# Softmax denominators of a causal self attention: summed on GpSimd and multiplied once a group

## The chip, the cores and the metric

The kernel runs on one core of one Trainium2 chip. The metric is the device time of one execution in microseconds (us). The engines are named as the profile names them: PE (TensorE, matmuls; PEld are its weight loads), DVE (VectorE), ACT (ScalarE), POOL (GpSimd) and SP (SyncE, which issues DMAs).

## The reference, cut to what matters

The reference is a two-layer Perceiver-like block on x of 512 rows by 512 columns. Each layer is a cross attention to 8192 context rows, a self attention over the 512 rows and a mixture of eight experts. The change touches the first layer's self attention alone:

```python
def _L0_attn_ref(x, w_qkv, b_qkv, w_out, b_out):
    ...
    qkv = x @ w_qkv + b_qkv
    q, k, v = jnp.split(qkv, 3, axis=-1)
    ...
    scores = jnp.einsum('bhid,bhjd->bhij', q, k) * attn_scale
    scores = jnp.where(j >= i, scores, -jnp.inf)
    attn = jax.nn.softmax(scores, axis=-1)
    out = jnp.einsum('bhij,bhjd->bhid', attn, v)
    out = out.transpose(0, 2, 1, 3).reshape(B, S, H)
    return out @ w_out + b_out
```

There are 16 heads of 32 columns. Query row i sees the keys j >= i only. The softmax needs, for each query and head, the sum of the weights exp(score - maximum) over its keys: the denominator.

## The kernel before

All is in 32-bit floats. The 16 heads are worked in four groups g of four heads (GH), the 512 keys in four tiles of 128. `self_attention0` works the tiles of a group in places i = 0 to 3, where place i holds key tile t = 3 - i. Since a query sees only keys at or behind it, tile t serves the queries 0 to (t + 1) * 128, so the widths w at places 0 to 3 are 512, 384, 256 and 128.

The steps of a group are closures. An order written out by hand, the string given to `in_order`, says which step's instructions are emitted next; each engine then works its own queue in order. A scheduler may still shift single instructions a little against this order.

- **q, k** (`query`, `key`, L1612 and L1616): projections on PE, with ACT adding the bias.
- **M g.t** (`maxima`): scores of a query tile on PE (L1683, and the causal mask added by a matmul at L1688), then on DVE the row maxima (L1692). **S** (`shift_of`) makes of them the shifts (DVE L826 and L829, PE transposes L835, DVE copy L839).
- **W g.i** (`weighted`): for four heads the scores with keys along partitions (PE L1670) and the shift subtracted by a small matmul (L800); ACT takes the exponentials into the tile pT (L1714); POOL sets the weights above the diagonal to zero in the last 128 columns (`affine_select`, L1716). Then it calls `sums` for the place before.
- **sums** (L1704): the matmuls of the weights of one place. With the values as weights loaded on PE they add to `acc`, with a matrix of ones (`ones32`) to `den`. The four heads of a batch write four blocks of 32 partitions. `acc` and `den` are one PSUM bank each, for the whole group; the places accumulate there.
- **F g** (`finish`): `sums` of the last place, then on ACT a copy of `acc` to `o` (L870) and the logarithm of `den` to `d` (L872).
- **D g** (`quotient`): ACT exp(-d) (L876), POOL o times d (L877), ACT adds the value bias (L880).
- **O g.j** (`outputs`): the output projection of two query tiles (PE L889), added to x by DVE (L895).
- **V** (`part`): a piece of another stage's work, the value projection of the second cross attention (PE L1548, ACT copy L1553). These pieces are spread through the order.
- **E, T**: group 3 is worked by query tiles and not by key tiles. It keeps its own denominators (L1743) in both kernels.

The tile pT has four buffers. PSUM has eight banks: six rotate among all short-lived tiles, scores, projections and transposes (`tile_s`: a new tile waits until the sixth before it has been read), and `acc` and `den` hold one each.

The part of the order that matters here (W0.2 is place 2 of group 0):

```python
"q0 k0 q1 M0.0 k1 M0.1 V M0.2 M0.3 q2 S0.0 M1.0 k2 M1.1 V S0.1 W0.0 M1.2 V W0.1 M1.3 "
"W0.2 W0.3 F0 S1.0 q3 D0 M2.0 M2.1 V S1.1 k3 M2.2 W1.0 O0.0 M2.3 W1.1 O0.1 "
"M3.0 V W1.2 M3.1 W1.3 F1 S2.0 M3.2 V D1 M3.3 S2.1 V W2.0 W2.1 S3.0 W2.2 "
"O1.0 W2.3 F2 S3.1 D2 O1.1 W3.0 V W3.1 V E3 O2.1 W3.2 V O2.0 E2 T3 W3.3 E1 T2 V E0 T1 "
```

Of the kernel before, what the change touches and what calls it, by code (L numbers as in the profile page):

```python
# [11 lines left out]
F32 = mybir.dt.float32  # L12
# [4 lines left out]
AF = mybir.ActivationFunctionType  # L17
ALU = mybir.AluOpType
# [3 lines left out]
P = 128  # L22
S = 512
D = 512
H = 16
HD = 32
S2 = 8192
NT = S // P
NC = D // P
NG = 4  # L30
GH = 4
# [3 lines left out]
E = 8  # L35
# [30 lines left out]
def tile_perceiver(  # L66
# [5 lines left out]
    nc = tc.nc  # L72

    def tile_pool(**kw):

        return tc.tile_pool(reuse_waits="tile", **kw)
# [38 lines left out]
    with tile_pool(name="begins", bufs=1) as tmp, tile_pool(name="beginsps", bufs=1, space=PSUM) as tps:  # L115
        t = tmp.tile([1, NCHUNK, CH // P], F32, name="brow")
        nc.gpsimd.iota(
            t, pattern=[[NC * CH // P, NCHUNK], [1, CH // P]], base=0, channel_multiplier=0,
# [11 lines left out]
    for i in range(2):  # L130
        t = const.tile([P, NT, GH, HD], BF16, name=f"mparts{i}")
# [9 lines left out]
    steps = const.tile([P, S], F32, name="steps")  # L141
# [21 lines left out]
    for i, caps in enumerate((CAPS0, CAPS1)):  # L163
        t = const.tile([P, 2, E], F32, name=f"rooms{i}")
# [5 lines left out]
    for i, name in enumerate(("L0_ffn_router", "L1_ffn_Wg")):  # L170
        t = const.tile([P, NC, E], F32, name=f"router{i}")
# [729 lines left out]
    def in_order(order, steps, k):  # L901


        shifts = {}
        for step in order.split():
            name, *n = step[0], *[int(v) for v in step[1:].split(".") if v]
            if name == "S":
                g, i = n
                if i == 0:
                    shifts[g] = k.shift_of(g)  # L910
                shifts[g][i]()
            elif name == "D":
                k.quotient(*n)
            elif name == "O":
                k.outputs(n[0], range(2 * n[1], 2 * n[1] + 2))
            else:
                steps[name](*n)
# [685 lines left out]
    def early_turns(k, tiles, to):  # L1603

        for t in tiles:
            turn(None, None, t, to, 0, held=True, tp=k.tile_s((P, NC, P), "lnt"))
# [11 lines left out]
    def self_attention0(pool, to, ahead=None):  # L1618
        with ExitStack() as st:
            psum = st.enter_context(tile_pool(name="s0ps", bufs=3, space=PSUM))  # L1620
            pacc = st.enter_context(tile_pool(name="s0acc", bufs=1, space=PSUM))
# [14 lines left out]
            vN = pool.tile([P, NT, D], F32, name="vNs", tag="vNs", bufs=1)  # L1636
            k = in_quads(pool, psum, pacc, qT, lambda: wo, bv, lambda: pool)
            k.rowwise = "whole"
            k.last = 0
            k.between = lambda: early_turns(k, (3, 2), to)  # L1640
            last = []

            def query(g):
                project(k, lambda c: wq[:, c, g * P : (g + 1) * P], xnT, 0, qT[:, g, :], bq[:, g : g + 1], SCALE)
# [19 lines left out]
            def scores(g, i):  # L1664
                t = NT - 1 - i
                w = (t + 1) * P
                tiles = [k.tile_s() for _ in range(GH)]
                for h in range(GH):
                    r = slice(HD * h, HD * (h + 1))
                    nc.tensor.matmul(  # L1670
                        tiles[h][:, 0:w], lhsT=kT[r, g, t * P : (t + 1) * P], rhs=qT[r, g, 0:w],
                        start=True, stop=False,
                    )
                for h in range(GH):
                    k.subtract(g, h, tiles[h][:, 0:w], w)
                return tiles, w
# [17 lines left out]
            def sums():  # L1694

                if not last:
                    return
                g, i, w, pT = last.pop()
                if i == 0:
                    k.begin(g)  # L1700
                t = NT - 1 - i
                for what in range(2):
                    for h in range(GH):
                        nc.tensor.matmul(  # L1704
                            k.sums[g][what][HD * h : HD * (h + 1), 0:w],
                            lhsT=k.ones32 if what else vN[:, t, g * P + HD * h : g * P + HD * (h + 1)],
                            rhs=pT[:, h, 0:w], start=(i == 0), stop=(i == NT - 1),
                        )

            def weighted(g, i):  # L1710
                tiles, w = scores(g, i)
                pT = pool.tile([P, GH, S], F32, name="pT", tag="pT", bufs=4)
                for h in range(GH):
                    nc.scalar.activation(pT[:, h, 0:w], tiles[h][:, 0:w], AF.Exp)  # L1714

                nc.gpsimd.affine_select(  # L1716
                    out=pT[:, :, w - P : w], in_=pT[:, :, w - P : w], compare_op=ALU.is_ge, fill=0.0,
                    base=0, pattern=[[0, GH], [-1, P]], channel_multiplier=1,
                )
                sums()  # L1720
                if g < NG - 1:
                    last.append((g, i, w, pT))
                else:
                    pTs[NT - 1 - i] = pT

            def finish(g):
                sums()
                k.finish(g)

            pTs = {}  # L1730

# [18 lines left out]
            def tail(t):  # L1750
                k.outputs(NG - 1, (t,))

            in_order(
# [5 lines left out]
                {"q": query, "k": key, "M": maxima, "W": weighted, "F": finish, "E": end, "T": tail, "V": part}, k,  # L1759
            )  # L1760

    def self_attention1(pool, to):

        W = S + 2 * PAD
        with ExitStack() as st:
# [75 lines left out]
            def finish(g):  # L1841
# [13 lines left out]
                k.finish(g, 2 if g == NG - 1 else 1)  # L1855

            in_order(
                "q0 k0 M0 q1 S0.0 k1 S0.1 M1 q2 S0.2 S1.0 W0 k2 S1.1 M2 F0 S1.2 q3 D0 S2.0 W1 "
                "k3 S2.1 M3 F1 S2.2 O0.0 D1 S3.0 O0.1 W2 S3.1 F2 O1.0 S3.2 D2 O1.1 W3 "
# [787 lines left out]
    def rest_of_layer0(full=False, **ahead):  # L2647
        self_and_ffn(
            "l0", self_attention0, full, a["L0_ffn_W1"], a["L0_ffn_W2"], 2048, 0, silu, False,
            CAPS0, tuple(reversed(range(NT))), **ahead,  # L2650
        )
# [34 lines left out]
    with tc.If(n > SLOTS):  # L2686

        load_x()
        with tile_pool(name="osb", bufs=1) as op:
            for i in range(2):  # L2690
                o = op.tile([P, S], F32, name=f"osb{i}", tag=f"osb{i}")
# [5 lines left out]
        with tile_pool(name="osb1", bufs=1) as op:  # L2697
            for i in range(2):
                o = op.tile([P, S], F32, name=f"osb1{i}", tag=f"osb1{i}")
# [113 lines left out]
```

## Time and profile before

| what | value |
|---|---|
| median of 3 runs | 1437.43 us (1436.31 to 1438.1) |
| the profiled execution | 1435.61 us, its span 1433.7 us, granted TensorE clock 0.993 |
| the stage of the change | about 448 to 532 us of the span |
| PE, ACT, POOL busy in those 84 us | 82.31, 34.81, 13.31 us |
| matmuls of L1704 in the trace | 96 for `acc`, 96 for `den`, 24 of each width |
| idle time of PE and of its weight loads before `acc`, ended by L1716 | 3.7 us, in 6 waits |

The span runs from the first to the last instruction of the profiled execution, and times within the trace count from its start. PE works a 32-bit matmul in two passes, so one matmul of the code is two records in the trace: a batch of four heads shows as eight. The matmuls of four heads in different blocks of the array overlap, which is why a batch of eight records of 0.6 us takes less than 1 us. The chain of waits gives the time that each piece took on the way to the end.

### The profile page before, as it was taken

The page shows a single profiled execution, that of the slowest core. Times are in us where ns is not written, and L with a number is a line of the kernel's source. Part 1 is how long each engine was busy: PE and PEld are TensorE (multiplying, and loading weights), DVE is VectorE, ACT ScalarE, POOL GpSimd, SP SyncE. Part 2 cuts the span into 40 slices and gives each one's busy share as a digit, 9 for nine tenths or more (in the row PEclk, how much of TensorE's full clock was granted, in tenths as well). Part 3 has the DMA queues.
Part 4 walks back from the last instruction along what each step waited for, and adds up shares of the span by engine and source line. Part 5 has one row for each costly group of instructions (what it writes and reads, how often), then busy time and mean ns, then how long its engine had stood idle before and what let it go on. Part 6 is the DMA issues. An engine that isn't in the chain of part 4 may idle for free.

```text
span 1433.7 us, 24957 instructions
## 1 busy us (share of the span) xinstructions
PE 1401.6 (98%) x9797; PEld 860.4 (60%) x9797; DVE 695.5 (49%) x1983; ACT 583.1 (41%) x1168; POOL 425.2 (30%) x359
## 2 busy tenths in 40 slices
PE   7989999999999999999999999999999999999997
PEld 3434444443244558999999766644444235499993
DVE  5558598985523424111111226769886525741112
ACT  2657466667732353111111131157667732321221
POOL 2150078987010110200001110058988010020002
PEclk9999999999999999999999999999999999989999
DMA  8455200000050005987889451000000050068575
GB/s 249 153 190 150 74 31 1 1 2 1 2 212 1 16 16 186 389 307 263 273 280 298 160 174 30 30 1 1 2 1 2 1 191 1 2 237 328 197 248 184
DMA packets 94267, 175.15 MB, mean 122 GB/s; under 512 B 5496, under 2 KB 32182, under 8 KB 92348
## 3 DMA queue, kind: packets, MB, share of 16 engines
q1 hardware_dynamic: 87004, 151.43, 31.5%
q0 software_dynamic: 6416, 19.94, 3.9%
q10 hardware_dynamic: 720, 2.10, 0.4%
q8 instruction: 79, 1.29, 0.4%
q14 instruction: 48, 0.39, 0.1%
HBM read 162.72 MB, written 9.68 MB: 120 GB/s over the span
## 4 chain that ended last, share of the span: by engine, by line
PE 88%; DVE 2%; ACT 1%; DMA 1%; issue 1%; POOL 0%; POOLq 0%; ACTq 0%
PE hps L2364 12%; PE y L2385 12%; PE sc L939 11%; PE acc L1044 8%; PE prj L1612 4%; PE pk L1421 4%; PE ops L889 4%; PE scm L957 4%; PE sc L957 3%; PE pv L1233 3%; PE den L1072 3%; PE pva L1548 2%; PE sc L800 2%; PE pk L1233 1%; PE y L2342 1%; PE pv L1457 1%
## 5 line engine op out<-in xcount | busy, mean ns | idle before, releaser
L1089 ACT ACTIVATE pT<-sc,kbias 128x512 f32<-128x512 f32 x480 | 288.3, 708 | 96.2 <-PE sc L800 85.7
L968 DVE CUSTOM_DVE_ANT_0 masked<-scm,krowb 128x512 f32<-128x512 f32 (+2 forms) x400 | 213.9, 591 | 40.0 <-PE scm L957 38.1
L939 PE MATMUL sc<-qTf,kTf 32*128 32x512 f32 x960 | 216.8, 621 | 1.5 <-DVE tops L968 1.5
L2364 PE MATMUL hps<-tokens,w 128*128 128x160 f32 (+11 forms) x1408 | 193.3, 293 | 0.0
L957 PE MATMUL scm<-kTf,qTf 32*128 32x512 f32 (+2 forms) x800 | 189.3, 539 | 0.0
L2364 PEld LDWEIGHTS hps<-tokens,w 128*128 128x128 f32 x1408 | 184.1, 191 | 2.7 <-issue 1.0
L2385 PE MATMUL y<-hT,w 128*128 128x160 f32 (+11 forms) x1280 | 176.2, 296 | 0.0
L2385 PEld LDWEIGHTS y<-hT,w 128*128 128x128 f32 x1280 | 169.7, 192 | 2.5 <-issue 0.8
L1063 POOL TENSOR_TENSOR four<-four,pT 128x2048 f32<-128x2048 f32 x36 | 163.9, 4553 | 1.6
L939 PEld LDWEIGHTS sc<-qTf,kTf 32*128 32x128 f32 x960 | 73.6, 183 | 95.7 <-DVE tops L968 42.5
L1044 PE MATMUL acc<-pT,vNf 128*32 128x512 f32 x960 | 127.8, 604 | 0.0
L968 DVE CUSTOM_DVE_ANT_0 masked<-sc,krowb 128x512 f32<-128x512 f32 (+2 forms) x176 | 98.6, 614 | 55.8 <-PE sc L957 55.2
L1063 POOL TENSOR_TENSOR four<-pT 128x2048 f32<-128x2048 f32 x24 | 109.3, 4554 | 54.1 <-ACT pT L1089 54.1
L2623 DVE TENSOR_TENSOR hT<-sg,hps 128x264 f32<-128x264 f32 (+7 forms) x64 | 28.0, 437 | 191.7 <-ACT sg L2622 177.1
L2622 ACT ACTIVATE sg<-hps 128x264 f32<-128x264 f32 (+7 forms) x64 | 25.3, 396 | 174.5 <-PE hps L2364 169.7
L957 PEld LDWEIGHTS scm<-kTf,qTf 32*128 32x128 f32 x800 | 86.1, 184 | 15.5 <-issue 6.3
L800 PE MATMUL sc<-shift,ones 3*128 3x512 bf16 (+3 forms) x544 | 93.2, 367 | 0.0
L2416 POOL DMA_DIRECT2D answers_d<-yb x17 | 9.6, 564 | 240.8 <-ACT yb L2403 240.8
L1052 DVE TENSOR_TENSOR o<-o,acc 128x512 f32<-128x512 f32 x84 | 57.3, 682 | 20.4 <-PE acc L1044 20.4
L1044 PEld LDWEIGHTS acc<-pT,vNf 128*32 128x32 f32 x960 | 19.3, 108 | 70.3 <-DVE tops L968 34.7
L1233 PE MATMUL pv<-wkvf,cslot 128*128 128x512 f32 x120 | 55.6, 613 | 3.0 <-issue 1.9
L1421 PE MATMUL pk<-cslot,wkf 128*128 128x256 f32 (+1 forms) x256 | 55.5, 370 | 0.0
(390 smaller groups left out, 1828.8 us busy)
## 6 DMA issues: line engine op xcount, KB each, us to landing
w<-in_L_ffn_W SPq DMA_DIRECT2D x94, 1024.0 KB, 6.6
mi<-in_mask SPq DMA_DIRECT2D x32, 512.0 KB, 4.2
cslot<-in_ctxT SPq DMA_DIRECT2D x40, 256.0 KB, 3.3
answers_d<-yb POOLq DMA_DIRECT2D x13, 256.0 KB, 4.6
answers_d<-zero POOLq DMA_DIRECT2D x9, 256.0 KB, 3.0
wkvf<-in_L_xattn_WkvT SPq DMA_DIRECT2D x8, 256.0 KB, 6.6
wof<-in_L_xattn_WoT SPq DMA_DIRECT2D x2, 1024.0 KB
wide<-in_L_attn_wk SPq DMA_DIRECT2D x4, 512.0 KB, 5.6
```

Of the source, the lines that this page charges most:

```text
L800: nc.tensor.matmul(ps, lhsT=ones16[r, :], rhs=k.shifts[g][r, 0:w], start=start, stop=stop)
L889: nc.tensor.matmul(ps, lhsT=k.o[g][:, t * P : (t + 1) * P], rhs=wo()[:, g, :], start=not direct, stop=True)
L939: nc.tensor.matmul(ps, lhsT=kT[HD * h : HD * (h + 1), g, i * P : (i + 1) * P], rhs=qT[HD * h : HD * (h + 1), g, :], start=True, stop=stop,)
L957: nc.tensor.matmul(ps[:, at : at + w], lhsT=qT[HD * h : HD * (h + 1), g, t * P : (t + 1) * P], rhs=kT[HD * h : HD * (h + 1), g, lo : lo + ...
L968: nc.vector.tensor_tensor_reduce(masked[:, 0:w], ps[:, at : at + w], krow[:, lo : lo + w], 1.0, -BIG, ALU.add, ALU.max, accum_out=tops[g % ...
L1044: nc.tensor.matmul(acc[HD * h : HD * (h + 1), :], lhsT=vN[:, i, g * P + HD * h : g * P + HD * (h + 1)], rhs=pT[:, h, :], start=alone or i ...
L1063: engine.tensor_tensor(to, parts[g][-1], pT, ALU.add)
L1089: nc.scalar.activation(pT[:, h, :], ps, AF.Exp, bias=kbias[:, i : i + 1])
L1233: last = nc.tensor.matmul(ps.rearrange("p (g n) -> p g n", g=NG), lhsT=src[:, c, s % 2, :], rhs=wkv[:, :, c, i * P : (i + 1) * P], start=( ...
L1421: end = nc.tensor.matmul(ps[:, j], lhsT=wk[:, g, c], rhs=src[:, c], start=(c == 0), stop=(c == NC - 1))
L2364: end = nc.tensor.matmul(ps[:, j, 0:k], lhsT=w1[:, c, f * P : (f + 1) * P], rhs=tokens[:, c, starts[r] : starts[r] + k], start=(c == 0), s ...
L2385: nc.tensor.matmul(accs[0][:, d, 0:k], lhsT=w2[:, f, d * P : (d + 1) * P], rhs=hT[:, f, 0:k], start=(c == 0 and f == 0 and d % 2 == 0), st ...
```

## The change

In groups 0 to 2 the weights of places 1 to 3 are added on POOL to the weights of place 0 (the tile kept as `total[g]`), which are overwritten by the sum. `sums` then multiplies by the values alone. The denominators are one batch of four matmuls of the ones with the sum, 512 wide, in the new step `divide`, which takes over the name D in the order; it also takes the logarithm on ACT, which `finish` did before, and then calls `quotient`. The denominators' PSUM tile comes from the six rotating banks; the bank that `den` had is not used. Group 3 and the other attentions stay as they are; `in_order` calls the new step where a caller brings one.

```diff
-            elif name == "D":
+            elif name == "D" and "D" not in steps:
                 k.quotient(*n)
...
                 if i == 0:
-                    k.begin(g)
+                    k.sums[g] = pacc.tile([P, S], F32, name="acc", tag="acc")
+                    total[g] = pT
                 t = NT - 1 - i
-                for what in range(2):
-                    for h in range(GH):
-                        nc.tensor.matmul(
-                            k.sums[g][what][HD * h : HD * (h + 1), 0:w],
-                            lhsT=k.ones32 if what else vN[:, t, g * P + HD * h : g * P + HD * (h + 1)],
-                            rhs=pT[:, h, 0:w], start=(i == 0), stop=(i == NT - 1),
-                        )
+                for h in range(GH):
+                    nc.tensor.matmul(
+                        k.sums[g][HD * h : HD * (h + 1), 0:w],
+                        lhsT=vN[:, t, g * P + HD * h : g * P + HD * (h + 1)],
+                        rhs=pT[:, h, 0:w], start=(i == 0), stop=(i == NT - 1),
+                    )
...
                 sums()
+                if 0 < i and g < NG - 1:
+                    to = total[g][:, :, 0:w]
+                    nc.gpsimd.tensor_tensor(to, to, pT[:, :, 0:w], ALU.add)
...
             def finish(g):
                 sums()
-                k.finish(g)
+                k.o[g] = pool.tile([P, S], F32, name="o", tag="o", bufs=2)
+                nc.scalar.copy(k.o[g], k.sums[g])
+
+            def divide(g):
+                den = k.tile_s(name="den")
+                for h in range(GH):
+                    nc.tensor.matmul(
+                        den[HD * h : HD * (h + 1), :], lhsT=k.ones32, rhs=total[g][:, h, :], start=True, stop=True
+                    )
+                k.d[g] = pool.tile([P, S], F32, name="d", tag="d", bufs=1)
+                nc.scalar.activation(k.d[g], den, AF.Ln)
+                k.quotient(g)
```

In the order that the changed kernel is built with, POOL's queue holds in groups 0 to 2, after the selections of places 0 and 1, the addition of place 1, the selection of place 2, its addition, the selection of place 3, its addition, and then the product of step D. On PE the batch of denominators stands behind the third projection matmul batch of q3 in group 0, behind a piece V in group 1, and in group 2 directly behind `acc` of place 3, between the two matmuls of O1.1. On ACT the logarithm of group 0 stands behind the bias of q3 and that of group 1 behind the copy of a piece V, which both stood behind step D before.

More of the change, by code (lines that the diff above doesn't have):

```diff
@@ L1640, in self_attention0 @@
             k.between = lambda: early_turns(k, (3, 2), to)
-            last = []
+            last, total = [], {}
             def query(g):
@@ L1758, in self_attention0 @@
                 "T0",
-                {"q": query, "k": key, "M": maxima, "W": weighted, "F": finish, "E": end, "T": tail, "V": part}, k,
+                {
+                    "q": query, "k": key, "M": maxima, "W": weighted, "F": finish, "D": divide, "E": end, "T": tail,
+                    "V": part,
+                }, k,
             )
```

## The prediction

> **What bounds the kernel now.** I read the page first: busy times and the shares of the chain of waits, then the row of the nearest Pool addition.
>
> ```profile
> PE 1401.6 (98%) x9797; PEld 860.4 (60%) x9797; DVE 695.5 (49%) x1983; ACT 583.1 (41%) x1168; POOL 425.2 (30%) x359
> ...
> PE 88%; DVE 2%; ACT 1%; DMA 1%; issue 1%; POOL 0%; POOLq 0%; ACTq 0%
> ...
> L1063 POOL TENSOR_TENSOR four<-four,pT 128x2048 f32<-128x2048 f32 x36 | 163.9, 4553 | 1.6
> ```
>
> TensorE (PE) sets the end nearly everywhere, so a matmul taken away is worth its place on the chain, and any wait put into PE's queue costs its full length. The stage that changes runs from about 448 to 532 us. There PE is busy 82.31 of 84.00 us, Pool 13.31. Next the chain of waits through group 0 (start, length, work), where each batch of four heads is one piece:
>
> ```profile
> 455.00 0.99 PE acc L1704 x8
> 456.00 0.86 PE den L1704 x8
> ...
> 459.62 0.65 PE den L1704 x8
> ...
> 460.76 0.62 PE acc L1704 x8
> 461.38 0.43 PE den L1704 x8
> 461.81 1.05 PE prj L1612 x2
> 462.87 0.36 PE acc L1704 x8
> 463.22 0.22 PE den L1704 x8
> 463.44 2.77 PE prj L1612 x6
> 466.21 1.07 PE sc L1683 x8
> ```
>
> A batch of denominators (den) takes 0.86, 0.65, 0.43 and 0.22 us on the chain at widths 512, 384, 256 and 128. Then Pool's own timeline in groups 0 and 2 (L1716 is the causal selection; I call those of a group s0 to s3, by the key tile's place i):
>
> ```profile
> 456.73 0.64 POOL L1716 TENSOR_SCALAR_AFFINE_SELECT pT<-pT 128x512 f32<-128x512 f32 x1 [3.85 <-ACT pT L1714]
> 460.05 0.63 POOL L1716 TENSOR_SCALAR_AFFINE_SELECT pT<-pT 128x512 f32<-128x512 f32 x1 [2.69 <-ACT pT L1714]
> 461.63 0.63 POOL L1716 TENSOR_SCALAR_AFFINE_SELECT pT<-pT 128x512 f32<-128x512 f32 x1 [0.94 <-ACT pT L1714]
> 465.20 1.26 POOL L877 TENSOR_TENSOR o<-o,d 128x512 f32<-128x512 f32 x1 [2.93 <-ACT d L876]
> ...
> 508.65 0.63 POOL L1716 TENSOR_SCALAR_AFFINE_SELECT pT<-pT 128x512 f32<-128x512 f32 x1 [1.02 <-ACT pT L1714]
> 511.72 0.64 POOL L1716 TENSOR_SCALAR_AFFINE_SELECT pT<-pT 128x512 f32<-128x512 f32 x1 [2.43 <-ACT pT L1714]
> 515.12 0.63 POOL L1716 TENSOR_SCALAR_AFFINE_SELECT pT<-pT 128x512 f32<-128x512 f32 x1 [2.77 <-ACT pT L1714]
> ```
>
> What to see: s1, s2, s3 start only 3.3 and 1.6 us apart in group 0 and 3.1 and 3.4 us in group 2, each as soon as its exponentials end, and PE follows at once (s3 ends 515.75, acc starts 515.81). Pool's idle time between them is short, though Pool as a whole is idle.
>
> **What is removed.** The dens of places 1 to 3: 0.65 + 0.43 + 0.22 = 1.30 us a group, 3.9 for three. The 512-wide batch moves from place 0 to step D; as a first batch of its kind it costs 0.99 (acc at 455.00) and not 0.86. Net 1.17 a group, 3.5 in all, if nothing waits.
>
> **What is added.** Three Pool additions a group, of 4 x 384, 4 x 256 and 4 x 128 elements per partition. The trace has no addition of that strided shape. Two rows of the same operation give the line: 4.553 us at 2048 (L1063), 1.265 at 512 (L877), so 2.14 ns an element and 0.17 fixed: 3.46, 2.36, 1.26 us. In Pool's queue each stands before the next selection: s1, add1, s2, add2, s3, add3. So s2 and s3, for which PE waits in acc, now stand behind additions for which nobody is in a hurry. About 0.1 us more passes where an instruction needs the result just before it (L1084 ends 251.14, L1086 starts 251.25).
>
> **Group 0** (times of the profiled run). s1 456.73 to 457.37; its exponentials lie ahead of the first den and don't move. add1 457.47 to 460.93; s2 to 461.56; add2 461.67 to 464.03; s3 to 464.66; add3 to 466.03. PE comes to acc of place 2 at 460.74 - 0.86 - 0.65 = 459.2 and waits 2.4 us, till 461.6. The matmul of prj queued behind it ends near 463.2, and PE waits 1.5 us more for s3. acc of place 3 runs 464.72 to 465.08, the rest of prj takes 2.77, D 0.99 (add3 is done by then): the next scores (M2.0, the piece at 466.21) start at 468.84. Group 0 loses **2.6 us**.
>
> **Group 1** has room: between s1 (484.45) and s2 (491.86) lie ops, scores and pva. add1 ends 488.7; s2, earlier by the den of place 0, runs 491.0 to 491.6, add2 to 494.1; the exponentials of place 3 end at 495.56 - 1.51 = 494.05, so s3 ends near 494.85, when PE gets there (496.79 - 1.94 = 494.85). The net 1.17 is kept. The pva behind D also waits no more for ACT's vNf copy (idle 0.3 at 501.50): that copy stood behind the bias step L880 and now goes ahead of Ln, and the pva takes the bank that Ln frees, about 0.1 before PE arrives. Gain **1.5**.
>
> **Group 2.** s1 508.65 to 509.28, add1 509.39 to 512.85, s2 to 513.48. PE, earlier by 0.86 + 0.65, has done acc, ops and scores by 512.7, waits 0.8, and does acc 513.54 to 514.10, the transposes of shifts and one ops till 515.3. add2 513.59 to 515.95, s3 to 516.58: acc of place 3 runs 516.64 to 517.0, after 1.3 us of waiting. add3 ends 517.95, D runs 518.01 to 519.0, behind it the second ops (0.95), and W3.0 starts at 519.95, not 518.39: 1.56 late. Behind D hangs one thing more: Ln, Exp, Pool's product and the bias took 516.86 to 520.23 on ACT and Pool; now 519.2 to 522.6, and the exponentials of W3.0 stand behind them in ACT's queue, 2.4 late. W3.1 needs the banks that they free, its last head at 524.15 where PE would be at 523.4: 0.75 more. Group 2 loses **2.3 us**.
>
> Sum: +2.6 - 1.5 + 2.3 = **+3.4 us**. PE's queue behind it is one chain to the end (the FFN's first list of rows and its DMA hang on the last pva), so I let nothing absorb it. ACT gains no instruction; SP's queue and all DMAs stay as they are; the freed PSUM bank is used by nobody; the den tile takes a turn among the six rotating banks, which the steps above include. The span is 1433.7 and its run 1435.61; the shift is put on the median, 1437.43 (runs 1436.31 to 1438.1): **1440.8 us**.
>
> **The unknown price, both ends.** Below: the selection itself, one input, 635 ns for 512, gives additions of 1.9, 1.3 and 0.63; then group 0 loses nothing (-0.1), group 2 gains about 1.0, the sum is -2.6, 1434.8. Above: Pool's dearest row for 512 elements, L1086, 1.58 us, is 1.25 times L877; add1 and add2 then push s3 later by 1.45 in groups 0 and 2 and D by 0.3 more in group 2, and some 0.4 in group 1: about +7.0, 1444.4. I take the same operation's own rows.
>
> **The clock.** What long waits do to the granted clock, from the table of stretches (seventh number: PEclk; first: length, then PE busy):
>
> ```profile
> 88.90:92.30 3.40, 0.00 (x0) 0.00 (x0) 0.03 (x1) 3.10 (x10) 0.59 (x3) 1.00 0.10 5
> 92.30:99.10 6.80, 6.08 (x16) 2.70 (x17) 5.60 (x16) 5.47 (x14) 0.43 (x2) 0.51 0.86 255
> 1157.30:1160.80 3.50, 1.67 (x12) 1.43 (x12) 1.99 (x6) 1.41 (x5) 0.00 (x0) 1.00 0.99 408
> 1160.80:1164.20 3.40, 3.40 (x12) 1.53 (x10) 2.99 (x7) 1.64 (x6) 1.27 (x2) 1.00 1.03 413
> ```
>
> 3.4 us without PE work were followed by 6.8 at half clock; 1.67 busy of 3.5 were not. Group 0 after the change has about 1.0 busy of the 3.4 from 459.2, in between. [...] By the rows the answer is open, so it is a rival.
>
> **Rivals.** (a) Half clock after group 0's wait: 6.8 us at half cost up to 3.4, less what falls into the second wait, say 2.7: 1443.5. For it: the first pair of rows; against: the second. (b) Faster: Pool's additions stay out of the way, PE keeps its 3.5: 1433.9. It decides from additions of about half my price, where s2 and s3 meet PE on time. For it: Pool is 30% busy; against: both rows of the same operation. (c) Part of the delay is won back, by waits in groups 0 and 2 some 15% shorter or by slack behind the stage (PE waits 0.91 and 0.53 for rows at 585 us): about +1.2, 1438.6.
>
> **How the numbers follow.** Forecast 0.54 (own range 1439.4 to 1442.2), (a) 0.26, (c) 0.12, (b) 0.08. A measurement of this kernel can tell about 0.2%, 2.9 us, from no change. The forecast lies just above it: 0.44 of its 0.54 is slower, 0.10 within; (a) is slower, (c) within, (b) faster. So slower 0.70, same 0.22, faster 0.08. The range runs from 1437.8, a little under (c), to the upper bound of Pool's price, 1444.5; (b) is left out.
>
> **What would show it.** Right: Pool additions of about 3.5, 2.4 and 1.3 us; acc of places 2 and 3 in groups 0 and 2 released by the selection after idle times of 0.8 to 2.4 us; none in group 1; exponentials of W3.0 held by the bias step. Wrong: PE's waits for L1716 staying under 1 us in all, or the den at D waiting long in groups 0 and 1; a stretch near 463 us at clock 0.5 is (a).

## The result and the profile after

| | median of the runs | profiled execution | its span |
|---|---|---|---|
| before | 1437.46 us (1436.31 to 1440.54, 17 runs) | 1435.61 us | 1433.7 us |
| after | 1441.13 us (1438.37 to 1446.36, 17 runs) | 1441.13 us | 1439.2 us |

The ratio is 1.0019, 95% interval 1.001 to 1.0028: by it the changed kernel is 2.7 us slower (1.4 to 4.0). It isn't the quotient of the medians, which lie 3.7 us apart, within the interval. The predicted 1440.8 us lies 0.3 us under the median, and the median within the range.

The page of the changed kernel, busy times and shares of the chain:

```profile
PE 1401.0 (97%) x9725; PEld 857.3 (60%) x9725; DVE 703.6 (49%) x1983; ACT 584.4 (41%) x1168; POOL 446.4 (31%) x368
...
PE 88%; DVE 2%; POOL 1%; DMA 1%; ACT 1%; issue 1%; POOLq 0%; ACTq 0%
```

PE has 72 matmul records fewer, POOL nine instructions and 21.2 us of busy time more. The share of POOL in the chain of waits rose from 0 to 1%. Pool's timeline in groups 0 and 2 (start, length, instruction) shows five of the nine additions, at L1723:

```profile
457.98 0.64 POOL L1716 TENSOR_SCALAR_AFFINE_SELECT pT<-pT 128x512 f32<-128x512 f32 x1 [3.85 <-PE sc L1688]
458.69 3.43 POOL L1723 TENSOR_TENSOR pT<-pT 128x1536 f32<-128x1536 f32 x1
462.08 0.64 POOL L1716 TENSOR_SCALAR_AFFINE_SELECT pT<-pT 128x512 f32<-128x512 f32 x1
462.80 2.34 POOL L1723 TENSOR_TENSOR pT<-pT 128x1024 f32<-128x1024 f32 x1
465.09 0.64 POOL L1716 TENSOR_SCALAR_AFFINE_SELECT pT<-pT 128x512 f32<-128x512 f32 x1
465.81 1.27 POOL L1723 TENSOR_TENSOR pT<-pT 128x512 f32<-128x512 f32 x1
...
512.94 3.45 POOL L1723 TENSOR_TENSOR pT<-pT 128x1536 f32<-128x1536 f32 x1
516.34 0.64 POOL L1716 TENSOR_SCALAR_AFFINE_SELECT pT<-pT 128x512 f32<-128x512 f32 x1
517.06 2.35 POOL L1723 TENSOR_TENSOR pT<-pT 128x1024 f32<-128x1024 f32 x1
519.36 0.64 POOL L1716 TENSOR_SCALAR_AFFINE_SELECT pT<-pT 128x512 f32<-128x512 f32 x1
```

The selections s2 and s3 have no idle time in brackets any more: Pool comes to them straight from an addition. The chain of waits now runs through Pool (start, length, work):

```profile
457.98 0.65 POOL pT L1716
458.62 0.07 issue
458.69 3.43 POOL pT L1723
462.12 0.60 POOL pT L1716
462.72 0.04 issue
462.76 1.08 PE acc L1704 x8
463.85 2.01 PE prj L1612 x2
465.85 0.59 PE acc L1704 x8
466.44 4.11 PE prj L1612 x6
470.55 1.00 PE den L1737 x8
471.54 1.07 PE sc L1683 x8
```

Before the change this stretch was PE alone. PE's own timeline has the wait for s2 in brackets, 2.26 us, and none before `acc` of place 3:

```profile
462.76 1.08 PE L1704 MATMUL acc<-pT,vNs 128*32 128x256 f32 x8 [2.26 <-POOL pT L1716]
...
465.78 0.66 PE L1704 MATMUL acc<-pT,vNs 128*32 128x128 f32 x8
```

Look also at the lengths in the chain: two records of prj take 2.01 us, and took 1.05 before. The table of stretches (edges, length, busy time of PE, PEld, DVE, ACT and POOL, granted clock, DMA share, GB/s) shows why:

```profile
455.43:458.85 3.42, 3.42 (x43) 1.72 (x40) 0.88 (x4) 1.85 (x5) 0.79 (x2) 1.00 0.00 0
458.85:462.26 3.41, 1.65 (x25) 0.49 (x20) 3.36 (x2) 2.00 (x8) 3.41 (x2) 1.00 0.00 0
462.26:465.67 3.41, 2.90 (x10) 0.70 (x10) 3.27 (x3) 0.00 (x0) 3.33 (x3) 0.50 0.00 0
465.67:469.09 3.42, 3.42 (x12) 1.38 (x12) 1.36 (x2) 0.59 (x1) 1.32 (x2) 0.50 0.00 0
469.09:472.50 3.41, 3.41 (x20) 0.85 (x18) 0.00 (x0) 1.54 (x3) 0.00 (x0) 1.00 0.00 0
```

After the wait for s2, PE ran 6.83 us at half clock. So in this execution rival (a) came on top of the forecast's waits.

To see where a kernel wins or loses I compare landmarks on PE: group 0 is the time from the first scores of W0.0 to those of M2.0, group 1 from those of W1.0 to those of W2.0, group 2 from those of W2.0 to those of W3.0, and W3 from there to the first `accq` of group 3. "To the router" goes from the last `accq` to the first matmul of the experts' router (`lps`). All are differences to the profile of the kernel before.

| | group 0 | group 1 | group 2 | W3 | to the router | half clock from (us) within 455 to 600 |
|---|---|---|---|---|---|---|
| predicted | +2.6 | -1.5 | +1.56 | +0.75 | 0 | none |
| after | +4.07 | -1.69 | +1.50 | +0.58 | 0.00 | 462.26 |
| changed_again | +3.96 | -1.69 | +1.48 | +0.58 | 0.00 | 460.92 |

The rest of the two spans' difference of 5.5 us, 1.25 us before the stage and -0.2 behind it, lies where the two kernels are the same.

### The profile page after: what moved, and what is told of

Its sections match the earlier page's. It is cut to its first block, busy times and chain, and to the rows that moved or that the text cites. A ratio compares the mean times of both kernels' runs of the same rounds, so it can differ in the third digit from the quotient of the medians.

```text
span 1439.2 us, 24817 instructions
## 1 busy us (share of the span) xinstructions
PE 1401.0 (97%) x9725; PEld 857.3 (60%) x9725; DVE 703.6 (49%) x1983; ACT 584.4 (41%) x1168; POOL 446.4 (31%) x368
## 4 chain that ended last, share of the span: by engine, by line
PE 88%; DVE 2%; POOL 1%; DMA 1%; ACT 1%; issue 1%; POOLq 0%; ACTq 0%
PE hps L2381 12%; PE y L2402 12%; PE sc L939 11%; PE acc L1044 8%; PE prj L1612 4%; PE pk L1421 4%; PE scm L957 4%; PE ops L889 4%; PE sc L957 3%; PE pv L1233 3%; PE den L1072 3%; PE pva L1548 2%; PE sc L800 2%; PE pk L1233 1%; PE y L2359 1%; PE pv L1457 1%
```

## The experiments

### The changed kernel again

`changed_again` is the changed kernel without an edit.

> The changed kernel once more, for a second profile. Theory: the waits for Pool's selections are the same to 0.1 us (2.3 and about 1.5 us in group 0 at full clock); whether the half clock falls on group 0 may differ from execution to execution, since the granted clock changes on a grid of 3.41 us whose phase is not the program's. If it falls here too, the stage loses 4.4 us against before, if not about 3.0. Rival: the half clock is a fixed part of the change and shows every time.

It took 1439.53 us, 1.0017 (1.0006 to 1.0028). Its stage, in the table above, repeats that of the first profile to 0.11 us, half clock included. So this run alone doesn't tell the theory from its rival; `g0_only`, next, does.

### One group at a time

`g0_only`, `g1_only` and `g2_only` sum one group on Pool and leave the other two as before:

```diff
+            SUMMED = (0,)
...
-                if 0 < i and g < NG - 1:
+                if 0 < i and g in SUMMED:
                     to = total[g][:, :, 0:w]
                     nc.gpsimd.tensor_tensor(to, to, pT[:, :, 0:w], ALU.add)
...
                 sums()
+                if g not in SUMMED:
+                    k.finish(g)
+                    return
...
             def divide(g):
+                if g not in SUMMED:
+                    k.quotient(g)
+                    return
```

> Only group 0 is changed; groups 1 and 2 keep their denominators on PE. Theory (PE waits for selections that stand behind additions in Pool's queue): +2.6 us by waits, the acc of place 2 idle 2.3 us and that of place 3 about 1.5 us, and up to 1.5 more in executions where the half clock falls on the waits, so +2.6 to +4.1 against the kernel before. Rival D (the batch of denominators in its new place and the longer run of Ln, Exp, product and bias cost the time): at most +1.0, since D finds its sum ready here.

> Only group 1 is changed. Theory: no wait for a selection, PE saves 1.2 us and the 0.3 us wait for the copy of vNf goes: -1.5 us against the kernel before. Rival D: D costs as much here as elsewhere, so 0 or a little slower.

> Only group 2 is changed. Theory: +2.3 us, of it 1.5 by waits of acc of places 2 and 3 and of D for Pool, and 0.75 because the exponentials of W3.0 stand behind the late bias step. Rival D: +0.75 to +1.7, the wait at D and the exponentials alone, with no idle time before acc. No stretch of half clock in this stage, by either.

| | median, ratio to before | group 0 | group 1 | group 2 | W3 | to the router | half clock from |
|---|---|---|---|---|---|---|---|
| g0_only | 1444.96, 1.0053 (1.0037 to 1.0068) | +2.52 | 0.00 | +1.64 | 0.00 | +1.74 | 511.38, 593.30 |
| g1_only | 1439.24, 1.001 (0.9998 to 1.0022) | 0.00 | -1.69 | +1.56 | 0.00 | +1.26 | 507.00, 588.92 |
| g2_only | 1441.44, 1.0021 (1.0011 to 1.0031) | 0.00 | 0.00 | +1.56 | +0.58 | +1.25 | 596.50 |

In `g0_only` the clock was full in group 0, and both waits stand in PE's timeline:

```profile
462.01 0.64 PE L1706 MATMUL acc<-pT,vNs 128*32 128x256 f32 x8 [2.27 <-POOL pT L1718]
...
465.03 0.43 PE L1706 MATMUL acc<-pT,vNs 128*32 128x128 f32 x8 [1.32 <-POOL pT L1718]
```

The groups' own terms come out one by one and close to the forecast: +2.52, -1.69, and +1.56 with +0.58. But the totals don't add up to the changed kernel (`g0_only`, with six runs, lies 7.5 us above the kernel before, where 2.6 to 4.1 was expected), and two strange terms appear: group 2 loses 1.6 us in the two kernels where it was not touched, and all three lose 1.2 to 1.7 us on the way to the router, which the changed kernel doesn't. The first goes with a half-clock stretch at 507 to 515 us, the second with no half clock. Both are followed up below. From the router to the second layer all three profiles lose 2.2 to 2.4 us more, with the half clock that the table has from 589 to 597 us on.

### Without the additions

`no_additions` is the changed kernel but for one line; its denominators are then those of place 0 alone:

```diff
-                    nc.gpsimd.tensor_tensor(to, to, pT[:, :, 0:w], ALU.add)
+                    pass
```

> The changed kernel without its nine Pool additions: the denominators of groups 0 to 2 are then those of place 0 alone. Everything else of the change is there, the moved batch, the bank, the order. Theory: the additions carry the whole loss, so this one is faster than the kernel before by 3.0 to 3.7 us, the 3.5 of PE among it. Rival D: not faster than before, since D and its chain are still there.

It took 1434.14 us, 0.9971 (0.996 to 0.9981). Group 0 changed by -0.51, group 1 by -1.69, group 2 by +0.63 and W3 by -0.19, with a half-clock stretch from 506.5 us in group 2. PE's timeline in group 0 (idle time and its releaser in brackets):

```profile
460.56 0.64 PE L1704 MATMUL acc<-pT,vNs 128*32 128x256 f32 x8 [0.63 <-POOL pT L1716]
461.13 1.13 PE L1612 MATMUL prj<-xnT,wq 128*128 128x512 f32 x2
462.19 0.43 PE L1704 MATMUL acc<-pT,vNs 128*32 128x128 f32 x8
```

With the additions gone, the wait before `acc` of place 2 is 0.63 and not 2.26 us, and before that of place 3 there is none, where `g0_only` has 1.32. So the saving on PE is real (3.4 us by the medians) and the additions cost more than it: 0.9971 against 1.0019.

### Where q3 stands

If the waits are the loss, work that needs no selection can fill them. `q3_in_first_gap` moves the projection q3 in the order as shown; `q3_in_second_gap` puts it behind W0.3:

```diff
-                "W0.2 W0.3 F0 S1.0 q3 D0 M2.0 M2.1 V S1.1 k3 M2.2 W1.0 O0.0 M2.3 W1.1 O0.1 "
+                "W0.2 q3 W0.3 F0 S1.0 D0 M2.0 M2.1 V S1.1 k3 M2.2 W1.0 O0.0 M2.3 W1.1 O0.1 "
```

> The changed kernel with q3's projection ahead of the scores of W0.3, so that it lies in the first wait of group 0. Theory: PE is busy until the selection of place 2 is done, waits under 1.5 us for that of place 3, and group 0 loses about 1 us instead of 2.6; 1.6 us faster than the changed kernel by waits alone, and more by what half clock costs on the average, for no stretch at half clock may stand near group 0 here. Rival (the waits are nothing, the additions slow something else): no faster than the changed kernel.

> The changed kernel with all four matmuls of q3's projection ahead of acc of place 3 in group 0, not one. Theory: the second wait of group 0 (1.5 us) is filled, PE then waits 0.5 us at D for the last addition; group 0 loses 0.8 to 1.0 instead of 2.6 at full clock, so 1.7 us faster than the changed kernel. The first wait of 2.3 us stays, and with it the chance of half clock. Rival (half clock carries the loss in group 0): no more than 0.5 us faster than the changed kernel, since the first, longer wait is untouched.

With q3 in the first gap both waits of group 0 are gone, no half clock falls there, and the group costs +0.80 us; the median is 1438.06 us, 1.0006 (0.9992 to 1.002). With q3 in the second gap the wait for s3 is gone, but that for s2 stays at 2.26 us and half clock begins with it at 461.12, so q3 runs slowly (6.28 us, and 3.70 in the first gap) and the group costs +3.81; 1441.17 us, 1.0013 (1.0001 to 1.0025). The 1.7 us expected over the changed kernel did not come; beside the 1.0017 of `changed_again` the runs show no difference, as the rival had it. Of the two waits the first mattered more here, for its length and for the clock that followed it.

### The additions of groups 0 and 2 on VectorE

`additions_on_dve` leaves those of group 1 on Pool and puts the others on DVE, in group 0 one step later in its queue so that they don't hold up the row maxima:

```diff
+                while due:
+                    due.pop()()
...
-                    nc.gpsimd.tensor_tensor(to, to, pT[:, :, 0:w], ALU.add)
+                    add = lambda: (nc.gpsimd if g == 1 else nc.vector).tensor_tensor(to, to, pT[:, :, 0:w], ALU.add)
+                    if g == 0:
+                        due.append(lambda: pin(add()))
+                    else:
+                        add()
```

> The changed kernel with the additions of groups 0 and 2 on DVE (in group 0 one step later in DVE's order, behind the maxima of M1.3), those of group 1 on Pool as in the change. DVE's rows give 1.7, 1.2 and 0.65 us. Theory: the selections meet PE on time in all three groups; group 0 -0.5 us against the kernel before, group 1 -1.5, group 2 -0.7: about -2.7, faster than both kernels. Rival D: still about 1 us slower than before, as the batches at D are unchanged. Rival 'DVE is in the way': slower than before, if the reductions of the maxima come late.

The first addition of group 0 on DVE's timeline takes half of Pool's 3.43 us:

```profile
460.67 1.75 DVE L1725 TENSOR_TENSOR pT<-pT 128x1536 f32<-128x1536 f32 x1
```

Group 0 changed by -0.51 us, as with no additions at all, group 1 by -1.69. Group 2 and W3 together lost 1.67, with half clock from 509.1 us, and the way to the router 1.74 again. The median is 1437.41, 0.9996 (0.9984 to 1.0009), not the 2.7 us expected. Group 0's wait for the additions is avoided, and in this profile other losses take the gain; how much of them an execution without these half-clock stretches would have is not shown.

### The bank of the denominators

What the three single groups and the DVE version share is another number or order of tiles in the six rotating banks, since the den tile of step D takes a turn there. `g1_own_bank` and `g0_own_bank` are `g1_only` and `g0_only` with that tile in the bank that `den` had before:

```diff
-                den = k.tile_s(name="den")
+                den = pacc.tile([P, S], F32, name="den", tag="den")
```

> Only group 1 is summed on Pool, as in g1_only, but its denominators go to the bank of their own that they had before the change, so the six rotating banks serve the tiles after them in the order of the kernel before. Theory (the 1.26 us that g1_only lost between the tail of group 2 and lps came from the rotation, shifted by one tile, which made a pva wait for ScalarE): that stretch changes by under 0.3 us against the kernel before, group 1 still gives -1.7 us, and the median is about 1.3 us below g1_only beside its own kernel before, a ratio of 0.999 to 1.000. Rival (the loss belongs to the later landing of o1 and so to the addition itself): the stretch to lps is again 1.2 to 1.3 us longer.

> Only group 0 is summed on Pool, as in g0_only, its denominators in the old bank of their own. Theory: group 0 costs 2.5 us where the clock stays full through its two waits, and 3.8 to 4.1 us where a half-clock stretch begins in them; the stretch to lps, +1.74 us in g0_only, falls to under 0.3 us; the median is 2 to 4 us above before, under the 7.5 us of g0_only. Rival: the stretch to lps stays at +1.7 us, and with it the median near 1445 us.

| | median, ratio to before | group 0 | group 1 | group 2 | to the router | half clock from |
|---|---|---|---|---|---|---|
| g1_own_bank | 1434.22, 0.9978 (0.9966 to 0.9989) | 0.00 | -1.70 | -0.12 | 0.00 | none |
| g0_own_bank | 1441.43, 1.0019 (1.0009 to 1.0029) | +2.64 | 0.00 | 0.00 | 0.00 | 464.88 (3.4 us) |

The way to the router is back to 0.00 in both. The last piece V before it, on PE's timeline, in `g0_only`:

```profile
550.18 1.99 PE L1548 MATMUL pva<-wva,cslot 128*128 128x256 f32 x8 [1.47 <-ACT x L293]
552.01 1.18 PE L2215 MATMUL lps<-router,xnTf 128*128 128x8 f32 x10
```

and in `g0_own_bank`:

```profile
549.11 1.04 PE L317 MATMUL lnt<-ident,xn_all 128*128 128x128 f32 x8
549.98 1.89 PE L1548 MATMUL pva<-wva,cslot 128*128 128x256 f32 x8
551.71 1.51 PE L2215 MATMUL lps<-router,xnTf 128*128 128x8 f32 x13
```

One tile more in the rotation, and 80 us later this pva stands in line for a bank that ScalarE still reads, for 1.47 us; with the old bank it doesn't wait. That this is the rotation is shown for these two kernels by the one line that differs. The changed kernel has three tiles more and no such wait, so the prediction's sum is not touched by it. `additions_on_dve` has the same three tiles more and does have the wait, 1.48 us; that the order in which tiles are taken makes this difference is likely and was not tested.

The median of `g1_own_bank` lies 3.4 us under that of the kernel before, more than the 0 to 1.4 us that was expected and more than the 1.8 us of its landmarks. Its profiled execution is 1.9 us shorter than that of the kernel before, and that one was itself about 1.9 us under its kernel's median. What the rest of the median comes from is open.

### The parts that win

> Group 0's additions run on VectorE one step later, group 1's on Pool, group 2 is as before the change, and the denominators of the two summed groups go to the old bank of their own. If the parts add up: group 0 -0.5 us (as in additions_on_dve and no_additions), group 1 -1.7 us, group 2 and the stretch to lps 0, so 2.2 us in all: about 1435.2 us, a ratio of 0.9985. Rival (the parts do not add, since the waits of group 2 or those after it take back what is won, as the hoisted heads did in additions_on_dve): a ratio of 0.9995 to 1.0005.

`best_guess` has the additions of group 0 on DVE, those of group 1 on Pool, group 2 as before and the old bank for the denominators. It took 1436.04 us, 0.998 (0.9968 to 0.9993): group 0 -0.51, group 1 -1.69, to the router 0.00, but group 2, untouched, +1.46 with half clock from 510.79. By their intervals both it and `g1_own_bank` are faster than the kernel before and the changed one. The intervals don't tell them apart; the simpler one, group 1 alone, has the lower median.

### The clock in group 0's wait

> The changed kernel with one matmul more (128 x 384 columns, its result is read by nobody) in TensorE's wait for s2 in group 0; it takes about 0.8 us of the 2.26 us wait, so TensorE is busy in over half of any 3.4 us there. Theory (the 1.5 us by which group 0 cost more than 2.5 us come from half-clock stretches that begin because TensorE stands still in that wait): the clock stays at 1.00 from 455 to 475 us, group 0 costs 2.4 to 2.7 us as in g0_only where the clock was full there, and the median is 0.5 to 1.5 us below that of the changed kernel beside its own kernel before (ratio 1.0005 to 1.0015). Rival (the half clock falls there whatever TensorE does in the wait): a half-clock stretch of 3.4 or 6.8 us begins between 460 and 466 us again, as in four of the five profiles that had this wait, and group 0 costs up to 4.1 us.

The edit:

```diff
+                if g == 0 and i == 2:
+                    busy = pacc.tile([P, S], F32, name="busy", tag="busy")
+                    pin(nc.tensor.matmul(busy[:, 0:384], lhsT=wq[:, 0, 0:P], rhs=xnT[:, 0, 0:384], start=True, stop=True))
```

Its profile has full clock through group 0, which costs +2.51 us. PE's timeline there:

```profile
458.60 0.91 PE L1705 MATMUL busy<-xnT,wq 128*128 128x384 f32 x2
460.93 0.64 PE L1707 MATMUL acc<-pT,vNs 128*32 128x256 f32 x8 [1.42 <-POOL pT L1719]
461.50 1.12 PE L1612 MATMUL prj<-xnT,wq 128*128 128x512 f32 x2
463.95 0.42 PE L1707 MATMUL acc<-pT,vNs 128*32 128x128 f32 x8 [1.32 <-POOL pT L1719]
```

One profile without half clock could be chance, as `g0_only` had none either. But the starts of all half-clock stretches of an execution lie whole multiples of 3.413 us apart (in the changed kernel's profile 93.62, 462.26, 1267.81, 1284.88 and 1435.06: 108, 236, 5 and 44 steps; in that of the kernel before 92.38, 1259.74, 1280.22 and 1430.40: 342, 6 and 44). So each execution has a grid, and its position can be read even where nothing falls. With the edge of the grid taken that lies 7 to 10.4 us behind the start of group 0:

| profiles with the wait for s2 | edge behind the start of group 0 | half clock from the next edge |
|---|---|---|
| changed_again, q3_in_second_gap, after | 8.78, 8.92, 9.00 us | 6.8 us in each |
| g0_own_bank | 9.43 us | 3.4 us |
| g0_only | 7.68 us | none |
| pe_kept_busy | 8.89 us | none |

`pe_kept_busy` lay on the grid as the three profiles did that were slowed for 6.8 us, and was not. The kernel before has its edge at 9.00 us, no such wait, and full clock. So on this position of the grid it is what PE does in the wait that brings the half clock, by three profiles against one with the added matmul and one without the wait. The median, though, came out at 1441.58 us, 1.0041 (1.0025 to 1.0057): nothing was won. Its profile says where it was given back: with group 0 shorter by 1.56 us, the same grid fell otherwise on group 2, an edge 1.05 us behind the start of W2.0 and not 0.41 ahead of it. A half-clock stretch began there at 508.11 (group 2 cost +1.76 and not +1.50), and another at 590.03 among the experts, whose stretch up to the second layer took 2.07 us more than before, against 0.52 in the changed kernel's profile:

```profile
456.91:460.32 3.41, 2.61 (x29) 0.88 (x23) 3.31 (x2) 2.00 (x8) 3.41 (x2) 1.00 0.00 0
460.32:463.74 3.42, 1.70 (x10) 0.45 (x10) 3.25 (x4) 0.00 (x0) 3.34 (x3) 1.00 0.00 0
...
504.70:508.11 3.41, 2.78 (x24) 1.18 (x20) 0.00 (x0) 3.06 (x7) 0.63 (x1) 1.00 0.00 0
508.11:511.52 3.41, 3.41 (x24) 0.89 (x20) 0.00 (x0) 1.18 (x4) 2.35 (x2) 0.50 0.02 5
```

Seven runs and one profile don't settle whether all of the 1.0041 is that; it stays open.

## Why the prediction was right, point by point

**Pool's additions** were forecast at 3.46, 2.36 and 1.26 us from two rows of the same operation and took 3.43, 2.34 and 1.27. The price by the selection's row (1.9, 1.3, 0.63) and the one by the dearest row fall.

**Group 0**: +2.6 forecast from waits of 2.4 and 1.5 us. `g0_only` at full clock has 2.27 and 1.32 us and +2.52.

**Group 1**: -1.5 forecast, -1.69 to -1.70 in every profile in which it was summed on Pool. No `acc` waits there. The 0.2 more is in the pva behind D: it starts 0.71 us after the transposes ahead of it in the profile before (500.79 to 501.50) and 0.22 us after (504.95 to 505.17), so the wait for ACT's copy was worth 0.5 us, and the forecast had counted PE's idle time of 0.3.

**Group 2**: +1.56 forecast for the start of W3.0, +1.50 measured (+1.56 in `g2_only`), from waits of 0.77 before `acc` of place 2, 1.14 before that of place 3 and 0.92 before den:

```profile
517.03 0.64 PE L1704 MATMUL acc<-pT,vNs 128*32 128x256 f32 x8 [0.77 <-POOL pT L1716]
...
520.05 0.43 PE L1704 MATMUL acc<-pT,vNs 128*32 128x128 f32 x8 [1.14 <-POOL pT L1716]
521.40 1.06 PE L1737 MATMUL den<-pT,ones 128*32 128x512 f32 x8 [0.92 <-POOL pT L1723]
```

The exponentials of W3.0 behind the bias were forecast at 0.75 and cost 0.58. ACT's timeline after shows them in line:

```profile
522.59 0.60 ACT L1741 ACTIVATE d<-den 128x512 f32<-128x512 f32 x1 [1.38 <-PE den L1737]
523.22 0.63 ACT L876 ACTIVATE d<-d 128x512 f32<-128x512 f32 x1
525.23 0.72 ACT L880 ACTIVATE o<-o,L_attn_bv 128x512 f32<-128x512 f32 x1 [1.38 <-POOL o L877]
525.85 2.04 ACT L1714 ACTIVATE pT<-sc 128x512 f32<-128x512 f32 x4
```

**The sum**, +3.4, is at full clock 2.52 - 1.69 + 1.50 + 0.58 = +2.9 by the runs. The time moved by 2.7 by the ratio (1.4 to 4.0) and by 3.7 by the medians. The mechanism and each group's term were right to 0.3 us, but that the forecast came within 0.3 us of the median is in part luck: all terms were put a little too high, and half clock in group 0, which the forecast had left out, adds some 1.5 us in some executions.

**Nothing is absorbed behind the stage**: so it was, no landmark behind W3 takes anything back up to the experts. Rival (c) falls in its first form (the waits for selections were 4 to 12% shorter than forecast, not 15%) and finds nothing for its second.

**Rival (a)** was given 0.26 as the other case, with +2.7 us beside the sum. It happened in both profiles of the changed kernel and in that of `q3_in_second_gap`, by half in `g0_own_bank`, and not in `g0_only`. Three things in it were off. It isn't a case for the kernel but for an execution: the grid decides (with the whole wait of 2.26 us, none with its edge at 7.68 us and 6.8 us with it at 8.78 to 9.00). The two pairs of rows that it was weighed by look at PE's busy time, which the last section shows not to decide; the profile before has a third pair, 3.06 us busy of 3.40 from 1276.8 us with half clock behind it, that already spoke against it. And its price was 1.44 to 1.55 us (3.96 and 4.07 against 2.52), not 2.7: its first 3.4 us slow a prj that would only have ended in the second wait (`g0_own_bank`, with 3.4 us of half clock there: +2.64).

**Rival (b)**, faster at 1433.9 us, is what `no_additions` measured (1434.14 us) and so what the change would have brought if Pool's work stood in nobody's way.

## What to carry to other kernels

Pool, 30% busy before, had no room where the next instruction in its queue is one that PE waits for, since it worked that queue in order (`after`: the first addition of group 0 runs from 458.69 to 462.12 us, s2 starts at 462.08): in two groups additions for a sum that is needed late stood ahead of four selections that were needed at once, and turned a saving of 3.4 us into a loss of 3.7 (both by the medians). Count the room between the urgent instructions, group by group: the one group that had it (its selections start 6.6 and 3.2 us apart after the change, at 489.70, 496.27 and 499.44 us, and PE is busy elsewhere meanwhile) gained 1.7 us, and that part alone, with the denominators in their old bank, is faster than both kernels. And a tile moved to another pool of banks opened a wait of 1.47 us some 80 us behind it (`g0_only`): compare landmarks along the whole program, not only in the stage that was edited.

## What was not expected of the hardware

The granted clock differs between executions of one kernel, and the time with it. Of the 29 runs of the kernel before that were taken beside the single groups, the two with a granted clock of 0.990 or less average 1441.5 us, the three with 0.995 or more 1435.0. Half-clock stretches begin on the 3.413 us grid, whose position differs from execution to execution (8.78 us behind the start of group 0 in `changed_again`, 9.00 in `after`, the same kernel). Group 2 shows it best, since six of the 14 kernels have it as it was before. With the grid edge taken that lies within -0.9 to 2.5 us of the start of W2.0, in all 14 profiles:

| edge behind the start of W2.0 | profiles | half clock from the next edge | group 2, where its code is that of before |
|---|---|---|---|
| -0.52 to 0.01 us | 5 | none | 0.00 us (`g0_own_bank`) |
| 0.89 to 1.72 us | 6 | 3.4 us in each | +1.46 to +1.64 us |
| 1.97 to 2.48 us | 3 | none | 0.00 and -0.12 us |

The window ahead of such a stretch in `g0_only`, and the matmuls at its end:

```profile
507.97:511.38 3.41, 2.70 (x20) 0.96 (x20) 0.00 (x0) 3.38 (x8) 0.64 (x1) 1.00 0.00 0
511.38:514.79 3.41, 3.41 (x24) 0.90 (x16) 0.00 (x0) 0.15 (x1) 0.63 (x1) 0.50 0.02 5
...
510.69 1.30 PE L1706 MATMUL acc<-pT,vNs 128*32 128x512 f32 x8 [0.68 <-POOL pT L1718]
```

PE was busy for 2.70 of 3.41 us and was slowed; in `pe_kept_busy` a window with 1.70 busy of 3.42 us, from 460.32, was not. So it isn't the busy time of the records that decides. The matmuls in the slowed window are the scores, with 32 rows of the array, the shifts, with 3, and in its last 0.7 us `acc`, with 128 rows and 32 columns; those in the other are `acc` and prj, which uses 128 rows and 128 columns.

How much of the array is at work fits all 14 profiles far better. Give each PE record the time that its columns take at prj's pace (3.49 us for eight records of 512, `after` at 477.39, so 0.85 ns a column, about half of that in bf16, where four records of 128 columns take 0.24 us, `after` at 460.27), times the share of the 128 by 128 array that its form names: 1 for prj, a quarter for scores and for `acc`. From 12 us on the profiles have 5745 whole steps of the grid at full clock. The 65 that half clock followed hold at most 1.32 us of such work; of the other 5680 only 11 hold as little. In the profiles of the kernel before and of the changed kernel alone it is nine of 820 steps, with at most 1.20 us, and one of the other 811 that holds as little (1.12, from 496.40 us in `after`). By busy time the 65 reach up to 3.35 us. The slowed window of group 0 holds 0.94 us in the changed kernel's profile; the window at the same place in `pe_kept_busy`, which was not slowed, holds 1.64, of which the added matmul is 0.65. In group 2 the six slowed windows hold 0.86 to 1.23, and those of the other profiles 1.39 or more. This was read from the profiles afterwards; no run was made to test where the limit lies, and the 11 exceptions (nine from 490 to 502 us, two in group 0) are unexplained.

PE's waits that begin in the slowed windows shown are 2.26 us long in group 0 (`after`) and 0.68 us in group 2 (`g0_only`).

What this does to the experiments: one profile can be some 1.5 us long or short in each of these places, and the runs of the unchanged kernel alone spread from 1432.8 to 1442.1 us. A part worth 1 or 2 us is read from landmarks in profiles whose clock was the same there, and only its sign, over many runs, from the medians.
